# A convolution and attention stack on one Trainium2 core: feature tiles that rotate, images held as halves, and convolution dealt out by counted TensorE time

## The chip, the cores and the metric

The kernel runs on one core of a Trainium2 chip. The metric is the device time of one execution in microseconds. It is a single program with hand-ordered instruction streams: every engine executes its own instructions in the order in which the program emits them, and semaphores join the engines.

## The reference

The input `x` is 8 images of 32 x 32 pixels with 256 channels, in float32. Two layers follow.

Layer 0 normalises each image over 32 groups of channels and adds to `x` the concatenation of a 3 x 3 convolution (192 channels) and of attention with 8 heads of size 8 (64 channels). The logits have two relative terms, one by row and one by column, which come from tables of 63 vectors:

```python
logits = einsum('bnid,bnjd->bnij', q, k) + rel_w + rel_h      # 1024 x 1024 for each of 8 heads
attn   = einsum('bnij,bnjd->bnid', softmax(logits), v)
x      = x + concat(conv3x3(gn(x)) + conv_b, attn @ attn_w + attn_b)
```

Layer 1 normalises each token, adds single-head attention over the 1024 tokens (`U = 128`), normalises again, and adds a mixture of experts. Its router uses the mean over an image's normalised tokens, so that each image picks two of eight experts (256 to 512 to 256, exact gelu), followed by a layer norm.

```python
t = t + (softmax(Q K^T / sqrt(128)) V) W_o + b_o + ln(t)
t = t + ln(experts(ln(t), top 2 of softmax(mean(ln(t)) @ Wr + br)) + ln(t)) * gamma + beta
```

## The kernel before

The tokens of an image are held as 8 tiles of 128 tokens (`NT`). The first phase, some 2050 us long, does layer 0 and the attention of layer 1 for the eight images in a software pipeline. The second phase, from about 2060 us to the end, does the router and the experts, and the change does not touch it.

**Features.** Layer 0's attention is computed from 128-row feature tiles. The product of a key matrix `KM` (keys, and constant rows that pick a row and a column) with a feature tile `F` gives logits that contain both relative terms and minus the row maximum. `F` is a 2 MB tile put together by DMA from DRAM scratch: `fd` holds the queries and the column pieces, `fy` the row pieces. There are three buffers for such tiles, `F0`, `F1` and `F2`, each with room for one. They also serve as scratch for the queries (`scr`, in `queries`, L534 to L546) and for the normalised tokens, queries and keys of layer 1 (`nqk`, in `Second`).

**Units.** An image has four units (`Unit`): head group `g` by half of the queries. A unit loads `F` (L671 from `fd`, L675 from `fy`, on the SP queue), computes 32 score products (`score`, L690) with a maximum of each on DVE (L697), folds the maxima and sends them by DMA into the rows `R_M` of `F` (`fold`, `fold_in` L713, `fold_out` L724 on ACT's queue). Then it weighs: 32 products (`weigh`, L734) with an exponential on ACT each (L741), and for every four of them a product with the values (`gather`, L750). `settle` (L765) transposes the result.

**The main loop.** `first_layer(b)` runs over the 32 steps `s` of an image, eight for each unit, with four places `p` each: 128 places, one `weigh` at each. While a unit weighs, the next one scores, 4/3 products a place or 8/5 from place 5 in the last unit, where the next one is unit 0 of the next image. At `s == NT` (place 32) the whole of layer 1's attention of the image before (`second_layer`) runs between two places. `project` prepares it during the first unit.

**Filling.** At each place the loop calls `fill.send(us)`. It runs what was put off by `later` (`catch_up`), then one step of a chain of side work, each step ending in `yield None`, and then convolution matmuls (L625) up to a credit of `us`, each of which is entered at 0.36 us. `pace` divides the convolution still owed by the places left. A convolution belongs to one image and is done by Winograd-like transforms along a row: `combine` (L493 on DVE, L496 on POOL) makes the six transformed inputs `V`, and `convolve_pair` issues 12 matmuls for a pair of them, 72 for an image (two instructions in the trace for each). After a pair, ACT copies the result and DVE or POOL add it to the image tile `T`.

**Side work.** After place 32 the chain holds, in this order: `token_mean(b - 1)` (write of `T` to DRAM, statistics, and the sum of normalised tokens with DVE products L1089 to L1091 and matmuls L1096), `fetch(b + 1)` (load of the next image into `T`, then eight empty steps), and `normalise(b + 1)`. The last transposes the image (L385), takes group statistics, makes `base`, then the keys and queries `kq` (`pk`, L434, with L442 on DVE), splits them into two parts (L428 on ACT, L429 on POOL), writes `kd`, and waits until the loop has reached `s == 2 * NT` (`may_query`). Then come the copies of `queries`, the values (`pvv`, L460), and the relative pieces of `features`: four rows (products `prel`, L566, ACT copy L584, DVE remainder L587, two DMA writes of `fy` L589) alternating with four columns (L603, L604), and then the write of the columns to `fd` (L614). Keys of group 0 (L554) and `Unit(b + 1, 0)` follow. `combine` waits for place 88 (`may_combine`).

**Where each tile lies.** Unit 3 uses `F2`, the others use `F0` or `F1` by parity:

```python
self.F = f_tile("F", 2 if n == 3 else (b + n) % 2)
scr    = f_tile("scr", b % 2)
big    = f_tile("nqk", 2, FP)
```

`Unit(b, 2)` is made at place 32, `Unit(b, 3)` at place 48 (`s == NT + 4`), and `Unit(b + 1, 1)` at place 96.

Of the kernel before, what the change touches and what calls it, by code (L numbers as in the profile page):

```python
# [38 lines left out]
def kernel(  # L39
# [44 lines left out]
    all1 = all1.to_broadcast([P, P])  # L84
# [27 lines left out]
    with ExitStack() as ph:  # L112
# [11 lines left out]
        def load_image(b):  # L124
            t = work.tile([P, NT, C], FP, tag="T", name="T", bufs=2)
            for g in range(2):
                nc.sync.dma_start(
                    out=t[:, 4 * g : 4 * g + 4, :], in_=xt[b, g * 512 : g * 512 + 512].rearrange("(p k) c -> p k c", k=4)
                )
            return t  # L130

        ph.enter_context(tc.manual_schedule())
        T = {0: load_image(0)}
# [79 lines left out]
        nc.vector.tensor_copy(kqb, pkb[:, 0:1])  # L213
# [113 lines left out]

        class Fill:
# [11 lines left out]
            def catch_up(self):  # L340
                due, self.due = self.due, []
                for work in due:
                    work()
# [8 lines left out]
            def send(self, us):  # L352
                self.catch_up()
                self.step()
                self.left += us
# [18 lines left out]
        ready = {}  # L374

        def normalise(b):
# [5 lines left out]
            def turned(kc, g):  # L382
                tp = lg_tile("tpx")
                for k in range(4):
                    nc.tensor.transpose(tp[:, k:512:4], T[b][:, 4 * g + k, kc * P : (kc + 1) * P], ident)  # L385
                return tp

            for kc in range(KC):
                for g in range(2):
                    nc.vector.bn_stats(st[:, kc, g, :], turned(kc, g))  # L390
                    yield None
                nc.vector.bn_aggr(mv[:, kc, :], st[:, kc].rearrange("p q s -> p (q s)"))
# [3 lines left out]
            nc.tensor.matmul(pm[:, 0:KC], lhsT=gavg, rhs=mv[:, :, 0], start=True, stop=True)  # L396
# [9 lines left out]
            nc.tensor.matmul(pv[:, 0:KC], lhsT=gavg, rhs=dm[:, :, 0], start=True, stop=True)  # L406
# [20 lines left out]
            def split(c):  # L427
                nc.scalar.copy(kqh[:, 0, c], kq[:, c])  # L428
                nc.gpsimd.tensor_tensor(kqh[:, 1, c], kq[:, c], kqh[:, 0, c], ALU.subtract)  # L429

            for q in range(2):
                pk = lg_tile("pk")
                for kc in range(KC):
                    nc.tensor.matmul(  # L434
# [7 lines left out]
                nc.vector.tensor_scalar(kq[:, c], pk, kqb, kqs, ALU.add, ALU.mult)  # L442
                fill.later(lambda c=c: split(c))
                yield None
            yield None
            kd = kds[b % 2]
            nc.sync.dma_start(out=kd.rearrange("l p s -> p l s"), in_=kqb_[0:DK])
            ready[b] = kqb_
            yield None
            while b > 0 and (done[b - 1] < NT or not may_query.get(b)):  # L450
                yield None
            qs, qx = queries(b)
            nc.gpsimd.tensor_tensor(T[b], T[b], l0b.to_broadcast([P, NT, C]), ALU.add)
# [3 lines left out]
            pv = mi_tile("pvv").rearrange("p (j c) -> p j c", c=DK)  # L457
            for j in range(NT):
                for kc in range(KC):
                    nc.tensor.matmul(  # L460
                        pv[:, j, :],
                        lhsT=base[kc][:, j * P : (j + 1) * P],
                        rhs=qkvw[:, kc, 2 * DK : 3 * DK],
                        start=kc == 0,
                        stop=kc == KC - 1,
                    )
                if j % 2:
                    yield None
            v0[b] = work.tile([P, NT, DK], FP, tag="v0", name="v0")
            nc.vector.tensor_tensor(v0[b], pv, vb.unsqueeze(1).to_broadcast([P, NT, DK]), ALU.add)  # L470
            yield None
            yield from features(b, qs, qx)
            if b > 0:
                keys(b, 0)
            units[b, 0] = Unit(b, 0)
            while not may_combine.get(b):
                yield None
            yield from combine(b, base)

        may_query, may_combine, units = {}, {}, {}  # L480
# [46 lines left out]
        def queries(b):  # L527
            kqb_ = ready.pop(b)
            scr = f_tile("scr", b % 2).rearrange("p w h s -> p (w h s)")
            qs = scr[:, 0 : 2 * S].rearrange("p (g s) -> p g s", g=NG)  # L530
            qx = scr[:, 2 * S : 4 * S].rearrange("p (g s) -> p g s", g=NG)
            for g in range(NG):
                for i in range(4):
# [25 lines left out]
        def features(b, qs, qx):  # L559


            def piece(tab, src, q):
                pr = lg_tile("prel").rearrange("p (i g s) -> p i g s", g=NG, s=32)
                for n in range(8):
                    i = q * 8 + n
                    nc.tensor.matmul(  # L566
# [29 lines left out]
            def column(q):  # L596
                pr = piece(bws, qx, q)
                for g in range(NG):
# [5 lines left out]
                    fill.later(lambda ps=ps, hi=hi, lo=lo: nc.vector.tensor_tensor(lo, ps, hi, ALU.subtract))  # L604

            for q in range(4):
                row(q)
                yield None
                column(q)
                yield None  # L610
            for g in range(NG):
                dst = fds[b % 2][g][R_M * HG : (R_M + 64) * HG].rearrange("(l p) s -> p l s", p=P)
                for p in (slice(HG, 64), slice(64, P)):
                    nc.sync.dma_start(out=dst[p], in_=whole[g].bitcast(FP)[p])  # L614

        done = {}

        def convolve_pair(b, g, pair):
# [3 lines left out]
            for i, j in enumerate(pair):  # L622
                for dy in range(3):
                    for kc in range(KC):
                        nc.tensor.matmul(  # L625
# [8 lines left out]
            Tg = T[b][:, 4 * g : 4 * g + 4, 0:CO]  # L634
            if pair == (0, 5):
                nc.vector.tensor_tensor(Tg[:, 0:4:3], pc, Tg[:, 0:4:3], ALU.add)
                fill.catch_up()
                done[b] = 4 * g + 4
            else:
                mm = work.tile([P, 2 * CO], FP, tag="n", name="mm", bufs=2).rearrange("p (j o) -> p j o", j=2)  # L640
                nc.scalar.copy(mm, pc)  # L641

                def rest():
                    ms = work.tile([P, CO], FP, tag="ms", name="ms")
                    nc.vector.tensor_tensor(ms, mm[:, 0], mm[:, 1], ALU.add)
                    nc.vector.tensor_tensor(mm[:, 0], mm[:, 0], mm[:, 1], ALU.subtract)
                    sd = (ms, mm[:, 0])
                    if pair == (1, 2):
                        for k in range(2):
                            T2 = Tg[:, k:4:2]  # L650
                            nc.gpsimd.tensor_tensor(T2, T2, sd[k].unsqueeze(1).to_broadcast([P, 2, CO]), ALU.add)
# [221 lines left out]
        def fetch(b):  # L873
            T[b] = load_image(b)
            for _ in range(8):
                yield None
# [546 lines left out]
```

## Time and profile before

| what | value |
| --- | --- |
| median of 3 runs | 2538.64 us (2533.96 to 2553.05) |
| the profiled execution | 2547.53 us, its span 2545.8 us |
| mean granted TensorE clock | 0.916 |
| busy share: PE, DVE, ACT, POOL | 89%, 57%, 40%, 16% |
| DMA moved | 185.97 MB, mean 73 GB/s |
| one steady image (4), from its first weigh to the next image's | 242.6 us |
| its second layer, between places 31 and 32 | 50.1 us |

All times in what follows are microseconds of the profiled execution unless they are called medians. Its own time is 1.7 us more than its span, and 8.9 us more than the median. "Granted clock" is the share of full speed that TensorE's throttle allowed in a stretch. In a table of windows a busy share of PE near the window's length means only that a matmul was in flight: at a clock of 0.5 the same matmul is in flight for twice as long.

### The profile page before, as it was taken

The page shows a single profiled execution, that of the slowest core. Times are in us where ns is not written, and L with a number is a line of the kernel's source. Part 1 is how long each engine was busy: PE and PEld are TensorE (multiplying, and loading weights), DVE is VectorE, ACT ScalarE, POOL GpSimd, SP SyncE. Part 2 cuts the span into 40 slices and gives each one's busy share as a digit, 9 for nine tenths or more (in the row PEclk, how much of TensorE's full clock was granted, in tenths as well). Part 3 has the DMA queues.
Part 4 walks back from the last instruction along what each step waited for, and adds up shares of the span by engine and source line. Part 5 has one row for each costly group of instructions (what it writes and reads, how often), then busy time and mean ns, then how long its engine had stood idle before and what let it go on. Part 6 is the DMA issues. An engine that isn't in the chain of part 4 may idle for free.

```text
span 2545.8 us, 28672 instructions
## 1 busy us (share of the span) xinstructions
PE 2270.9 (89%) x10507; PEld 1455.8 (57%) x10507; DVE 1455.3 (57%) x3229; ACT 1010.4 (40%) x1921; POOL 404.7 (16%) x294
## 2 busy tenths in 40 slices
PE   5479999899989998999899989998998869999998
PEld 4346556556646654566556645655653546666665
DVE  4656766665757576666666666666563443333333
ACT  1144543444434444544443444344445312332222
POOL 2101120211021111201110112021100032222220
PEclk7788999799979997998899889989999879999999
DMA  5543412531271145024512351243120031221110
GB/s 133 120 84 101 91 34 67 134 57 34 70 170 17 34 112 137 10 52 107 123 39 64 95 105 34 67 124 68 34 51 2 0 121 66 75 75 66 66 58 25
DMA packets 91165, 185.97 MB, mean 73 GB/s; under 512 B 9313, under 2 KB 37866, under 8 KB 88466
## 3 DMA queue, kind: packets, MB, share of 16 engines
q1 hardware_dynamic: 89216, 181.55, 29.3%
q10 hardware_dynamic: 1810, 2.59, 0.4%
q8 instruction: 84, 1.38, 0.2%
q14 instruction: 55, 0.45, 0.1%
HBM read 112.15 MB, written 62.52 MB: 69 GB/s over the span
## 4 chain that ended last, share of the span: by engine, by line
PE 70%; DVE 14%; DMA 8%; ACT 3%; SPq 2%; issue 2%; POOL 1%; ACTq 0%; DVEq 0%; POOLq 0%
PE phd L1333 9%; PE py L1350 9%; PE st L734 8%; PE po L750 8%; PE lg L690 8%; PE pc L625 6%; DVE mx L697 5%; PE po L1051 4%; PE lg L973 4%; DMA F<-fy 3%; DMA F<-mb 3%; PE pq L847 2%; PE prel L566 2%; PE tp L997 2%; PE pa L1059 1%
## 5 line engine op out<-in xcount | busy, mean ns | idle before, releaser
L697 DVE TENSOR_REDUCE mx<-lg 128x1 f32<-128x512 f32 x1024 | 660.1, 684 | 375.5 <-PE lg L690 370.6
L741 ACT ACTIVATE PT<-st 128x512 f32<-128x512 f32 x1024 | 590.9, 597 | 572.6 <-PE st L734 518.6
L734 PE MATMUL st<-F,KM 128*128 128x512 f32 x1024 | 536.4, 530 | 55.3 <-ACT PT L741 34.5
L690 PE MATMUL lg<-KM,F 128*128 128x512 f32 x1024 | 400.8, 433 | 68.5 <-DMA F<-fy 64.8
L734 PEld LDWEIGHTS st<-F,KM 128*128 128x128 f32 x1024 | 208.9, 206 | 244.1 <-ACT PT L741 153.8
L750 PE MATMUL po<-PT,vk 128*32 128x512 f32 x2048 | 308.0, 673 | 0.7 <-POOL vk L871 0.7
L625 PE MATMUL pc<-convw,V 128*128 128x192 f32 x1152 | 283.5, 339 | 9.2 <-ACT mm L641 5.0
L625 PEld LDWEIGHTS pc<-convw,V 128*128 128x128 f32 x1152 | 206.2, 193 | 118.5 <-issue 71.4
L690 PEld LDWEIGHTS lg<-KM,F 128*128 128x128 f32 x1024 | 212.8, 208 | 101.1 <-issue 73.0
L1333 PE MATMUL phd<-n2T,w 128*128 128x512 f32 x512 | 225.4, 596 | 0.0
L1350 PE MATMUL py<-w,hT 128*128 128x256 f32 x1024 | 223.6, 379 | 0.0
L1350 PEld LDWEIGHTS py<-w,hT 128*128 128x128 f32 x1024 | 194.6, 190 | 33.3 <-issue 7.7
L1357 DVE TENSOR_TENSOR r<-py,n 128x256 f32<-128x256 f32 x64 | 27.2, 425 | 261.4 <-PE py L1350 261.4
L1333 PEld LDWEIGHTS phd<-n2T,w 128*128 128x128 f32 x512 | 96.2, 191 | 114.0 <-issue 110.3
L978 ACT ACTIVATE pr<-lg,nm 128x512 f32<-128x512 f32 x128 | 86.7, 683 | 127.4 <-DVE nm L975 127.2
L1340 ACT ACTIVATE hT<-phd,b1c 128x512 f32<-128x512 f32 x128 | 86.3, 686 | 96.6 <-PE phd L1333 96.5
L974 DVE TENSOR_REDUCE nm<-lg 128x1 f32<-128x512 f32 x128 | 86.5, 688 | 64.1 <-PE lg L973 64.1
L973 PE MATMUL lg<-nqk 128*128 128x512 f32 x256 | 120.9, 595 | 0.0
L1051 PE MATMUL po<-pt,v 128*128 128x256 f32 x512 | 115.8, 379 | 0.0
L429 POOL TENSOR_TENSOR kqh<-kq,kqh 128x512 fp32r<-128x512 f32 x16 | 20.4, 1275 | 557.6 <-ACT kqh L428 557.5
L828 POOL TENSOR_TENSOR T<-T,n 128x256 f32<-128x256 f32 x64 | 48.5, 777 | 369.0 <-DVE n L827 369.0
L1051 PEld LDWEIGHTS po<-pt,v 128*128 128x128 f32 x512 | 95.1, 190 | 11.6
(249 smaller groups left out, 2462.6 us busy)
## 6 DMA issues: line engine op xcount, KB each, us to landing
F<-fd SPq DMA_DIRECT2D x64, 768.0 KB
fy<-rel SPq DMA_DIRECT2D x64, 256.0 KB
F<-fy SPq DMA_DIRECT2D x128, 128.0 KB
w<-in_L_ffn_W_dram SPq DMA_DIRECT2D x32, 512.0 KB
T<-in_x_dram SPq DMA_DIRECT2D x16, 512.0 KB
scr<-kqh SPq DMA_DIRECT2D x64, 128.0 KB
fd<-kqh SPq DMA_DIRECT2D x32, 256.0 KB
fd<-rel SPq DMA_DIRECT2D x16, 512.0 KB
```

The source lines that it names most:

```text
L625: nc.tensor.matmul(pc[:, i], lhsT=V[j][:, kc, (16 * g + dy) * NQ : (16 * g + dy) * NQ + P], rhs=convw[:, j, dy * KC + kc], start=dy + kc == 0,
L690: nc.tensor.matmul(lg, lhsT=self.F[:, a, hl, i * P : (i + 1) * P], rhs=KM[:, self.g * HG + hl, a * 512 : (a + 1) * 512], start=True, stop= ...
L697: nc.vector.tensor_reduce(self.mx[:, a, i, hl : hl + 1], lg, AX.X, ALU.max, negate=True)
L734: nc.tensor.matmul(st, lhsT=KM[:, self.g * HG + hl, j * P : (j + 1) * P], rhs=self.F[:, j // 4, hl, :], start=True, stop=True,)
L741: nc.scalar.activation(self.pts[j][:, hl, :], st, AF.Exp)
L750: nc.tensor.matmul(self.po[32 * hl : 32 * hl + 32, :], lhsT=vk[:, j, (self.g * HG + hl) * (DH + 1) : (self.g * HG + hl) * (DH + 1) + 32], ...
L973: nc.tensor.matmul(lg[h], lhsT=q, rhs=k[:, h * 512 : (h + 1) * 512], start=True, stop=True)
L974: nc.vector.tensor_reduce(nm[:, h : h + 1], lg[h], AX.X, ALU.max, negate=True)
L978: nc.scalar.activation(pr[:, h * 512 : (h + 1) * 512], lg[h], AF.Exp, bias=nm[:, 2:3], scale=scale, accum_out=rs[:, h, i : i + 1],)
L1051: nc.tensor.matmul(po[:, 0:IB], lhsT=sec.v[:, jc, :], rhs=pt[:, jc, :], start=jc == 0, stop=jc == NT - 1)
L1333: nc.tensor.matmul(phd, lhsT=ws[k][0][:, kc, f * P : (f + 1) * P], rhs=n2T[:, kc, q * 512 : (q + 1) * 512], start=kc == 0, stop=kc == KC - 1,)
L1350: nc.tensor.matmul(py, lhsT=hT[:, k * NF + f, j * P : (j + 1) * P], rhs=ws[k][1][:, f, :], start=k + f == 0, stop=k == TOPK - 1 and f == N ...
```

## The change

1. **Roles rotate.** Of the three feature buffers, `place_of(b, role)` gives role 0 (scratch of the queries, units 0 and 2), role 1 (units 1 and 3) and role 2 (`nqk` of the image before) to another buffer in each image. The scratch for the next image's queries is thereby the buffer that `nqk` leaves at place 32. The waits `may_query` and `may_combine` go: the queries follow at once when the keys are made, and `combine` waits only until the image before has its convolution done. `Unit(b, 3)` is made at place 64, where unit 1 leaves its buffer, with the next image's keys of group 0 behind it. The score schedule follows: unit 3 is scored at 15/8 a place from place 7 of unit 2 on, and the next image's unit 0 at 11/8 from place 1 of unit 3 on.
2. **Halves.** `T` becomes two tiles of four token tiles each, with two buffers a half. The first half of the image after next is loaded when `token_mean` of half 0 is done, inside the second layer. `token_mean` runs once for each half, the first inside the second layer. Its constant term goes into the first DVE product in place of a matmul.
3. **Pieces.** The order is row, column, column, row, column, column, row, write of the columns, an empty step, last row, where rows and columns alternated. Two empty steps stand ahead of the first piece. The values use two `lg` tiles and not the convolution's `mi` tile.
4. **Counting.** `Counted` adds an estimate of TensorE's time for every matmul and transpose. `send(us, level)` gives the convolution the credit `level + us - spent`. The convolution is paced to end at place 66 of the image's own loop.
5. **Smaller moves.** The scaling of `kq` and one copy of `nqk` go from DVE to ACT, with the split in the same step. The copies of the queries are issued replica by replica. Adding a pair (3, 4) to `T` is spread over three sends.

```diff
+        class Counted:
+            spent = 0.0
+            def matmul(self, out, **kw):
+                n = math.prod(out.shape[1:])
+                us = max(n * (0.00046 if kw["rhs"].dtype == FR else 0.00168), 0.06)
+                self.spent += 0.31 * us if out.shape[0] == 32 else us
+                nc.tensor.matmul(out, **kw)
+            def transpose(self, out, in_, ident):
+                self.spent += 0.115
+                nc.tensor.transpose(out, in_, ident)
...
+        def load_half(b, g):
+            t = work.tile([P, 4, C], FP, tag=f"T{g}", name="T", bufs=2)
...
+        def place_of(b, role):
+            return (role - b) % 3
...
-            def send(self, us):
+            def send(self, us, level=None):
                 self.catch_up()
                 self.step()
-                self.left += us
+                self.left += us if level is None else max(level + us - te.spent, 0.0)
+                te.spent = 0.0
...
-                nc.vector.tensor_scalar(kq[:, c], pk, kqb, kqs, ALU.add, ALU.mult)
-                fill.later(lambda c=c: split(c))
+                nc.scalar.activation(kq[:, c], pk, AF.Identity, bias=kqb, scale=kqs)
+                nc.scalar.copy(kqh[:, 0, c], kq[:, c])
+                nc.gpsimd.tensor_tensor(kqh[:, 1, c], kq[:, c], kqh[:, 0, c], ALU.subtract)
...
-            while b > 0 and (done[b - 1] < NT or not may_query.get(b)):
-                yield None
             qs, qx = queries(b)
...
-            if b > 0:
-                keys(b, 0)
             units[b, 0] = Unit(b, 0)
-            while not may_combine.get(b):
+            while b > 0 and done[b - 1] < NT:
                 yield None
             yield from combine(b, base)
...
-            scr = f_tile("scr", b % 2).rearrange("p w h s -> p (w h s)")
+            scr = f_tile("scr", place_of(b, 0)).rearrange("p w h s -> p (w h s)")
...
-            for g in range(NG):
-                for i in range(4):
+            for i in range(4):
+                for g in range(NG):
...
-            for q in range(4):
-                row(q)
-                yield None
-                column(q)
-                yield None
+            for f, q in ((row, 0), (column, 0), (column, 1), (row, 1), (column, 2), (column, 3), (row, 2)):
+                f(q)
+                yield None
+            store_columns()
+            yield None
+            yield None
+            row(3)
+            yield None
...
-                self.F = f_tile("F", 2 if n == 3 else (b + n) % 2)
+                self.F = f_tile("F", place_of(b, n % 2))
...
-                big = f_tile("nqk", 2, FP).rearrange("p w h s -> p (w h s)")
+                big = f_tile("nqk", place_of(b + 1, 2), FP).rearrange("p w h s -> p (w h s)")
...
-        def fetch(b):
-            T[b] = load_image(b)
-            for _ in range(8):
+        def fetch(b, g, wait):
+            load_half(b, g)
+            for _ in range(wait):
                 yield None
...
-        def pace(b, s, p):
-            if done.get(b, NT) < NT:
-                left, later = 4 * (15 - s) - p, 5.0 if s < NT else 0.0
-            else:
-                left, later = 4 * (32 - s) - p + 24, 5.0
-            return max(fill.owed - later, 0.0) / max(left, 1)
+        LAST = 66
+        def pace(b, place):
+            left = (LAST if done.get(b, NT) < NT else 128 + LAST) - place
+            return fill.owed / max(left, 1)
...
+            starts = {2: lambda p: (p - 7) * 15 // 8, 3: lambda p: (p - 1) * 11 // 8}
+            starts[0] = starts[1] = lambda p: p * 4 // 3 + 1
...
                     if more:
-                        fill.chains.append(fetch(b + 1))
+                        fill.chains.append(fetch(b + 1, 1, 3))
                         fill.chains.append(normalise(b + 1))
-                elif s == NT + 4:
+                elif s == 2 * NT:
                     units[b, 3] = Unit(b, 3)
-                elif s == 2 * NT:
-                    may_query[b + 1] = True
-                elif s == 2 * NT + 6:
-                    may_combine[b + 1] = True
+                    if more:
+                        assert b + 1 in kept
+                        keys(b + 1, 0)
...
-                    fill.send(pace(b, s, p) * (0.6 if p == 1 else 1.13))
+                    fill.send(pace(b, 4 * s + p), 0.7)
...
+                    if ib % 2:
+                        fill.chains.append(token_mean(b, ib // 2, st2))
+                        if ib == 1 and b + 2 < B:
+                            fill.chains.append(fetch(b + 2, 0, 0))
...
-        def token_mean(b):
+        def token_mean(b, half, st2):
...
```

## The prediction

> **What bounds the kernel now.** I read the page first, then TensorE's timeline of one steady image cut at its score matmuls, then waits and the SP queue inside the bad stretches. From the page:
>
> ```profile
> PE 2270.9 (89%) x10507; PEld 1455.8 (57%) x10507; DVE 1455.3 (57%) x3229; ACT 1010.4 (40%) x1921; POOL 404.7 (16%) x294
> PEclk7788999799979997998899889989999879999999
> PE 70%; DVE 14%; DMA 8%; ACT 3%; SPq 2%; issue 2%; POOL 1%; ACTq 0%; DVEq 0%; POOLq 0%
> ```
>
> TensorE bounds it, but about every third slice its clock sags, and 8% of the chain is DMA. L734 runs 1024 times, 128 an image: I call each one a place. Image 4 lasts from 1034.3 to 1276.9, 242.6 us. Windows cut at places 0, 31, 32 (between them the second layer), 53, 64, 72, 81, 89, 96, 104 and 128; columns are length, then busy PE, PEld, DVE, ACT, POOL, granted clock, DMA share and GB/s:
>
> ```profile
> 1034.30:1082.60 48.30, 45.32 (x243) 27.46 (x242) 32.12 (x77) 24.02 (x47) 11.41 (x11) 1.00 0.08 13
> 1082.60:1132.70 50.10, 49.35 (x241) 36.10 (x240) 29.76 (x63) 19.57 (x50) 2.00 (x2) 1.00 0.22 43
> 1132.70:1161.30 28.60, 24.04 (x113) 14.97 (x112) 21.12 (x55) 12.78 (x24) 0.00 (x0) 0.88 0.57 147
> 1161.30:1173.70 12.40, 12.06 (x78) 7.22 (x76) 10.57 (x29) 6.16 (x14) 0.00 (x0) 1.00 0.01 4
> 1173.70:1187.80 14.10, 14.10 (x81) 9.01 (x79) 9.08 (x16) 6.78 (x12) 2.55 (x2) 1.00 0.28 62
> 1187.80:1213.80 26.00, 23.36 (x104) 17.62 (x103) 12.96 (x24) 9.13 (x19) 8.36 (x3) 0.64 0.49 128
> 1213.80:1223.30 9.50, 9.50 (x36) 4.52 (x36) 6.19 (x11) 4.71 (x10) 0.00 (x0) 0.72 0.79 230
> 1223.30:1232.50 9.20, 5.25 (x28) 1.72 (x27) 6.97 (x14) 4.33 (x8) 6.57 (x8) 1.00 0.89 188
> 1232.50:1246.80 14.30, 9.75 (x32) 4.21 (x33) 4.83 (x10) 4.74 (x9) 2.13 (x3) 0.64 0.94 193
> 1246.80:1276.90 30.10, 29.74 (x162) 19.54 (x161) 23.21 (x44) 14.83 (x27) 2.14 (x2) 1.00 0.14 24
> ```
>
> The reader sees three holes. Just after place 32, 4.6 us idle and a clock of 0.88 (the token mean's DVE burst). In places 72 to 89 the relative pieces run at 0.64 and 0.72. In 89 to 104 TensorE is idle 8.5 us while DMA is 0.9 busy. Busy time by clock over 960 to 1200 adds up to 202 of 240 us; 20 are idle, 18 are lost to the clock. Only these 38 us an image can be won. The waits from place 72 to 128 name what ends the last hole:
>
> ```profile
> PE lg L690 <- DMA F<-fy: 4.5, 1, 4.5
> PE st L734 <- DMA F<-mb: 2.6, 1, 2.6
> ```
>
> The SP queue shows why the features of the next image come so late: copies of the queries, relative pieces and both loads of F follow each other within 60 us.
>
> ```profile
> 1182.33 0.60 SPq L447 DMA_DIRECT2D kd<-kqh  x1
> 1183.03 6.98 SPq L534 DMA_DIRECT2D scr<-kqh  x8
> 1190.06 3.23 SPq L541 DMA_DIRECT2D fd<-kqh  x4
> 1216.09 4.78 SPq L614 DMA_DIRECT2D fd<-rel  x4
> 1224.87 8.12 SPq L671 DMA_DIRECT2D F<-fd  x2
> 1233.04 2.53 SPq L675 DMA_DIRECT2D F<-fy  x4
> ```
>
> **The change, stage by stage, one image.** I count the sends of the chain of side work, one a place. After place 32: five of the mean of half 1, load and three waits, then normalise. That puts the two key and query matmuls (pk) at places 52 and 53, the queries' copies at 55, the pieces at 59 to 65 and 68, and F of the next image's unit 0 at 69. Before, pk stands at 64 and 65, the pieces at 73 to 80, that F at 82. Thirteen places earlier; the price is that F of unit 3 is now asked for at place 64 and not 48, and that its scores (32 between places 72 and 89) meet the combination for the convolution, which now starts at 69 and not 88.
>
> *Places 0 to 31 and the second layer, 98.4 us.* TensorE is 94.7 busy at clock 1.00. Two copies of 0.69 us go from DVE to ACT, whose idle time covers them. Half 0's mean (4 products of 0.48 us, 4 aggregates, the inverse root) enters the second layer, where DVE has 20 us free; if a matmul waits for it, about 1 us. I take +1: 99.4.
>
> *32 to 53, 28.6 us.* Half 1's mean has half the DVE work: 4 x 0.15 + 4 x 0.48 us less, so ACT gets its inverse root about 2 us earlier and the 4.6 us hole closes to about 2, with less of the 2.9 us of lost clock. More convolution moves in: today image 4 has 30, 30, 26, 0 and 58 of its 144 instructions in 0-31, second layer, 32-64, 64-104 and 104-128; spread evenly some 6 matmuls of 0.32 us come here. Between 23.5 and 28; I take 25.5.
>
> *53 to 72, 26.5 us.* This stage gets dearer. From the second pk (1177.54) to the first piece (1192.28) took 14.7 us: product, split, then 9 to 10 us of SP issues and copies. That path stays, less one late send. TensorE has between them pk 1.9, five places of 0.24 to 0.55, 3.3 of pvv, 1.1 of po, 0.5 of pmx and about 4 convolution matmuls: some 10.4 us. So it waits 4 us, where it waited 2.1, and again 1.5 us for POOL's second copy (1.96 us each, both now start at the end of the copies). Eight pieces then cost 0.9 us each at full clock and 1.75 at half. With weigh, gather and ACT's 0.6 us a place, 72 is reached 43 us after 53 at half clock. At full clock it would be 31, but then F of unit 3, asked for about 23 us after 53 and 11.0 to 11.25 us in transfer (the two cold loads on the chain), holds the first score until 35. So 35 to 43. The wait before the pieces resembles the one that took the clock down in image 3, nearer the half-clock row:
>
> ```profile
> 960.00:965.00 5.00, 5.00 (x24) 3.66 (x17) 1.63 (x5) 1.18 (x2) 0.00 (x0) 0.50 0.11 38
> 965.00:970.00 5.00, 5.00 (x20) 4.51 (x20) 2.69 (x6) 1.18 (x3) 0.00 (x0) 0.50 0.33 108
> 970.00:975.00 5.00, 5.00 (x18) 2.50 (x18) 2.40 (x5) 2.33 (x6) 0.00 (x0) 0.50 0.47 148
> ```
>
> I take 38, as some places lie between the pieces now. (The Trainium skill, page TensorE: Matmul & The Clock Gate, section "Part 1: The HAM clock gate", says that one idle window of about 3.4 us halves the clock and one busy window of that length restores it. Its first half speaks against this change, which lengthens the wait at the first piece; its second half disagrees with these rows, where PE is fully busy for 15 us and stays at 0.50. By the rule the stage would be about 35 us and the kernel some 20 us faster than my sum; I follow the rows.)
>
> *72 to 89, 35.5 us.* The pieces are gone. DVE sets the pace: 32 maxima of 0.64 back to back are 20.5 us, the combination about 10.5 us (its 14 operations in image 4 last 0.42 to 0.94 us), of which 3 places fall before 72. 27 to 31; I take 29.5. TensorE's 17 places (some 17 us with 1.9 scores each, and convolution) hide under it.
>
> *89 to 96, 9.2 us.* The maxima's DMA (mb) meets a quieter queue: next F is asked for at 69, and 5.5 MB lie before it at about 200 GB/s, so it lands some 39 us after place 64; place 92 comes at about 43. ACT's 7 x 0.6 us and convolution: 6. *96 to 104, 14.3 us:* the wait for F goes, 8 places of about 1 us: 8. *104 to 128, 30.1 us:* 29 matmuls of convolution become about 11, 18 x 0.32 us less: 24.
>
> Sum 99.4 + 25.5 + 38 + 29.5 + 6 + 8 + 24 = 230.4, that is 12.2 us less an image, 85 for the seven that prepare a successor. Against it image 0: its successor's input is asked for behind a 2 MB F at place 32 and wanted at 35, not 43; 3 MB take about 14 us by the 11 us row, places 3 to 4: +9. At the end only half a mean is left: -4, half of the stretch 2040 to 2048. The renamed roles themselves, the flush, and 16 ACT products in place of DVE's cost nothing visible (ACT is 40% busy; without that cover 0.6 us each, 10 us). The profiled execution took 2547.5 us (span 2545.8), so 2467; the median of the runs is 8.9 lower: **about 2457 us**.
>
> **Rivals.** *All holes close.* If the convolution that is left fills the wait at place 58, the pieces keep the clock, and F of unit 3 is there at 72: 99 + 24 + 31 + 25.5 + 5.5 + 8 + 23 = 216, 26.6 less, so about 2360. For it: TensorE would be at 202 + 14 of real work, and 29 places lie between the request and the need of the next image's first F. Against: no work is put before the first piece on purpose, and unit 3's F has only 8 places.
>
> *Gain eaten.* The counter subtracts also the convolution sent at the place before, so credit comes only at every second place and what is left piles up before place 66, at half clock: the count does not spread evenly. If 53 to 89 takes 43 + 34 and the rest is as above, 240 an image: about 2530.
>
> *Slower.* One mechanism: the load of F for unit 3, on SP behind the writes of pieces 0 and 1, which wait for DVE, and sharing the DMA engines with 2.5 MB of pieces. TensorE is in order, so its first score at place 72 stops the weighing behind it, ACT then starves, and the combination is late next. In the forecast F lands 11 us after place 64. From about 12 us beyond that the gain is gone; at 17 us beyond (3 MB of other traffic ahead) an image costs 247, about 2575. For it: F<-fd took 8.12 us to issue twice and landed late when it followed the pieces. Against: there it waited for its own data, here the data lie in DRAM since the image before.
>
> **How the numbers follow.** Forecast (2415 to 2510) 0.55; all holes close (2340 to 2415) 0.18; gain eaten (2513 to 2564) 0.15; slower 0.12. One per cent, 25 us, is about what a measurement here can tell from no change. Faster 0.73, same 0.15, slower 0.12. The range 2375 to 2540 takes in the bounds of places 53 to 89 (35 to 43, 27 to 31) and leaves about 0.2 out.
>
> **What would show it.** Right: an image period near 230; no wait of lg for F<-fy at places 98 to 104; mb landing in 2 to 3 us; pieces some 13 places earlier, still with clock about 0.5; a wait of prel near 4 us; about two thirds of the convolution gone from 104 to 128 to other stages. Wrong: a clock near 1.0 through the pieces (then faster), or a wait of lg for F above 10 us in places 72 to 76 (then no gain).

## The result, and the profile after

The changed kernel takes 2648.25 us (median of 4 runs, 2638.23 to 2652.23) against 2544.52 for the kernel before: 1.040 times the time, 95% interval 1.035 to 1.046. The forecast was 2457 us. The kernel is about 104 us slower, and it was to be 87 us faster.

The page of the changed kernel (its profiled execution took 2638.23 us), the rows that answer to the three shown of before:

```profile
PE 2269.2 (86%) x10507; PEld 1450.2 (55%) x10507; DVE 1424.8 (54%) x3269; ACT 1035.4 (39%) x1969; POOL 396.2 (15%) x302
PEclk7796999799989988998899799989999879999999
PE 60%; DVE 22%; DMA 8%; ACT 3%; issue 3%; SPq 2%; ACTq 1%; POOL 1%; DVEq 0%; POOLq 0%
```

TensorE has the same matmuls and is busy for as long, so the 90 us of added span are idle time of TensorE. Image 4 of the changed kernel runs from 1081.1 to 1335.6, 254.5 us where it was 242.6. The same kind of windows, here cut at places 0, 31, 32, 53, 64, 72, 89, 96, 104 and 128:

```profile
1081.10:1130.30 49.20, 45.29 (x233) 26.58 (x233) 30.73 (x75) 24.62 (x47) 11.41 (x11) 0.97 0.07 12
1130.30:1187.10 56.80, 52.04 (x248) 37.97 (x246) 32.58 (x78) 20.38 (x52) 2.00 (x2) 0.97 0.25 56
1187.10:1217.30 30.20, 26.08 (x134) 15.52 (x133) 25.22 (x67) 13.07 (x26) 0.00 (x0) 0.94 0.11 36
1217.30:1249.10 31.80, 26.18 (x131) 18.96 (x129) 8.67 (x18) 11.40 (x21) 10.86 (x6) 0.72 0.44 104
1249.10:1269.80 20.70, 12.35 (x62) 8.32 (x63) 4.32 (x11) 6.87 (x14) 0.00 (x0) 0.75 1.04 244
1269.80:1293.90 24.10, 22.24 (x88) 11.04 (x88) 23.71 (x43) 10.20 (x18) 7.48 (x10) 0.87 0.57 133
1293.90:1302.10 8.20, 6.89 (x40) 3.45 (x38) 3.49 (x8) 3.77 (x7) 0.00 (x0) 1.00 0.01 4
1302.10:1310.40 8.30, 8.30 (x47) 5.40 (x48) 4.99 (x11) 5.83 (x11) 1.15 (x1) 1.00 0.87 200
1310.40:1335.60 25.20, 24.62 (x134) 14.79 (x132) 19.16 (x36) 14.02 (x25) 1.00 (x2) 1.00 0.15 20
```

Against the forecast: 106.0 for 99.4 up to place 32, 30.2 for 25.5, **52.5 for 38** in places 53 to 72, 24.1 for 29.5, 8.2 for 6, 8.3 for 8, and 25.2 for 24. Together the image misses its 230.4 us by 24.1. The late gains came for the most part (places 89 to 128 are down from 53.6 to 41.7, forecast 38). Two losses were not foreseen. Row five shows the first: 8.3 us of idle PE with DMA at 1.04. The waits of places 53 to 72, of PE and then of ACT, name it:

```profile
PE st L132 <- ACT PT L768: 8.4, 1, 8.4
PE prel L132 <- DMA scr<-kqh: 4.7, 1, 4.7
ACT rel L606 <- DMA fy<-rel: 9.1, 1, 9.1
```

Line 132 is the counting helper, so tiles tell the instructions apart. L606 is ACT's copy of a row piece. Its buffer is one of the three of `b_tile`, and `base` holds the other two, so the copy of row 3 waits until the write of row 2 has landed. The exponentials (L768) stand behind that copy, and TensorE waits for them. The SP queue shows what that write waits for:

```profile
1248.86 1.27 SPq L698 DMA_DIRECT2D F<-fd  x2
1250.17 2.71 SPq L702 DMA_DIRECT2D F<-fy  x4
1252.92 1.04 SPq L576 DMA_DIRECT2D KM<-kd  x2
1257.68 2.42 SPq L611 DMA_DIRECT2D fy<-rel  x2
1260.60 3.51 SPq L632 DMA_DIRECT2D fd<-rel  x4
```

Unit 3's F (L698, L702, 2 MB) and the keys are issued from 1248.86, and row 2's write (L611) at 1257.68, behind them. On the chain of work that ended last this is, in each of images 1 to 6, 10 to 11 us of F<-fd and then 7 to 9 us of fy<-rel. Where nothing stands ahead of it, the same write is 2.5 us on the chain (kernel before, at 57.69).

The second loss is in the second layer, 56.8 for 50.1 us. Its longest wait of PE is for half 0's sum:

```profile
PE pmean L132 <- DVE acc L1117: 2.8, 1, 2.8
```

### The profile page after: what moved, and what is told of

Same layout as the page of the kernel before. It is cut to its first block, busy times and chain, and to the rows that moved or that the text cites. A ratio compares the mean times of both kernels' runs of the same rounds, so it can differ in the third digit from the quotient of the medians.

```text
span 2636.4 us, 28742 instructions
## 1 busy us (share of the span) xinstructions
PE 2269.2 (86%) x10507; PEld 1450.2 (55%) x10507; DVE 1424.8 (54%) x3269; ACT 1035.4 (39%) x1969; POOL 396.2 (15%) x302
## 4 chain that ended last, share of the span: by engine, by line
PE 60%; DVE 22%; DMA 8%; ACT 3%; issue 3%; SPq 2%; ACTq 1%; POOL 1%; DVEq 0%; POOLq 0%
DVE mx L724 11%; PE po L132 11%; PE phd L1357 8%; PE py L1374 8%; PE lg L132 8%; PE st L132 7%; PE pc L132 4%; DMA F<-fd 3%; PE pq L132 2%; PE prel L132 2%; DMA fy<-rel 2%; PE tp L136 2%; SPq L556 1%; DVE V L515 1%; DMA F<-fy 1%
## 5 line engine op out<-in xcount | busy, mean ns | idle before, releaser
L768 ACT ACTIVATE PT<-st 128x512 f32<-128x512 f32 x1024 | 595.3, 597 | 521.5 <-PE st L132 480.5
L132 PE MATMUL st<-F,KM 128*128 128x512 f32 x1024 | 528.5, 521 | 76.8 <-ACT PT L768 75.9
L132 PEld LDWEIGHTS st<-F,KM 128*128 128x128 f32 x1024 | 202.8, 199 | 302.0 <-ACT PT L768 216.6
L132 PE MATMUL po<-PT,vk 128*32 128x512 f32 x2048 | 297.7, 653 | 0.0
L132 PEld LDWEIGHTS lg<-KM,F 128*128 128x128 f32 x1024 | 200.9, 197 | 136.0 <-issue 63.7
L132 PEld LDWEIGHTS pc<-convw,V 128*128 128x128 f32 x1152 | 215.4, 199 | 69.9 <-issue 23.9
L132 PE MATMUL po<-pt,v 128*128 128x256 f32 x512 | 129.8, 412 | 0.0
L132 PEld LDWEIGHTS po<-pt,v 128*128 128x128 f32 x512 | 105.6, 211 | 15.6
L609 DVE TENSOR_TENSOR rel<-prel,rel 128x512 fp32r<-128x512 f32 x32 | 22.1, 691 | 168.7 <-ACT rel L606 168.7
```

Source lines behind the costliest of these rows:

```text
L132: nc.tensor.matmul(out, **kw)
L768: nc.scalar.activation(self.pts[j][:, hl, :], st, AF.Exp)
```

## Experiments

Times of whole kernels are medians; each group ran beside its own runs of the kernel before (2541 to 2547 us). "A", "B" and "C" are the theory and its rivals in the text that stands ahead of each result. Images are numbered from 0.

**The load behind row 2's write.** `Unit(b, 3)` and the keys are made by the chain of pieces and not at the top of place 64:

```diff
+            if b > 0:
+                while not free.get(b - 1):
+                    yield None
+                units[b - 1, 3] = Unit(b - 1, 3)
+                keys(b, 0)
             store_columns()
...
-                    units[b, 3] = Unit(b, 3)
...
+                    free[b] = True
...
```

> The changed kernel with one step moved: F of unit 3 (and the keys behind it) is asked for two places later, behind the write of row piece 2 and ahead of the write of the columns. Theory A (order in the queue): in the changed kernel ACT's copy of row piece 3 waits 9.1 us for the buffer of row piece 2, whose write stands behind the 2 MB load of F; the exponentials queue behind that copy and TensorE starves. Then places 64 to 72 fall from 21 to 12 to 14 us, 72 to 89 rise by at most 3 (F lands later), an image costs 247 to 250 in place of 253 to 254, and the kernel 2590 to 2620 us. Rival B (DMA engines full): the engines are busy all through that stretch (share 1.04), so whatever goes first something else is late by as much; TensorE then waits for F at place 72 and the time stays within 10 us of the changed kernel's 2648.

2638 us. In image 4 places 64 to 72 fell to 13.5 us as A has it, and ACT's longest wait for fy<-rel fell from 9.1 to 2.1. But 72 to 89 rose to 36.2, with a new wait:

```profile
PE lg L132 <- DMA F<-fy: 11.1, 1, 11.1
```

So the order moves the wait and does not remove it, as B says for the time. B's reason does not hold: the DMA share there is 0.38 and then 0.77, not full. Asked for at place 64 or later, the load is late in either order.

**No load for unit 3.**

```diff
-                self.F = f_tile("F", place_of(b, n % 2))
+                self.F = units[b, 1].F if n == 3 else f_tile("F", place_of(b, n % 2))
...
+                if n != 3:
...
```

The loads of L698 and L702 stand under this `if`. The kernel leaves out unit 3's load, and with it that load's 2 MB of traffic.

> The changed kernel, where unit 3 loads no F: it scores and weighs with unit 1's tile, so its logits are those of other queries and the computation of that unit is changed. Theory A (the load asked for at place 64 and needed at 72 is too late, in whatever order it stands): without it ACT's wait of 9.1 us goes and no wait for F takes its place; places 64 to 72 take 11 to 13 us and 72 to 89 24 to 26, an image 244 to 247, the last one 193 to 196, the kernel 2575 to 2600 us. Rival B (the pieces' own cost, the wait for the queries' copies and half clock): 64 to 72 still takes 16 us or more, the kernel 2615 us or more.

2556 us, 93 less. Image 4 takes 239.6 us (images 1 to 6: 239.6 to 247.4), the last one 195.6 to its last weigh (204.7 before the edit; there unit 3's first score waited 7.0 us for F). By A, with somewhat more than it gave: ACT's longest wait for fy<-rel in image 4's stage is 2.9 us, and no score waits for F there.

**The old roles.** Buffers, unit 3 at place 48, start of the queries, place of the keys and pace of scoring as before:

```diff
-                self.F = f_tile("F", place_of(b, n % 2))
+                self.F = f_tile("F", 2 if n == 3 else (b + n) % 2)
...
-            starts = {2: lambda p: (p - 7) * 15 // 8, 3: lambda p: (p - 1) * 11 // 8}
+            starts = {2: lambda p: p * 4 // 3 + 1, 3: lambda p: (p - 5) * 8 // 5 + 1}
...
```

> The changed kernel with the roles of the feature buffers, the request for unit 3's F at place 48, the start of the queries at place 64, the place of the keys and the pace of scoring as they were before; halves, order of the pieces, count and the smaller moves stay. Theory A (the rotation is what hurts; the count is worth 25 to 40 us, half 0's mean costs 40): 2535 to 2565 us, 64 to 72 at 14 and 72 to 89 at 28 to 36. Rival B (halves and pieces hurt as much): 2600 us or more.

2501 us, ratio to before 0.985 (0.982 to 0.989). This group of edits, called the rotation below, costs 147 us; all the other parts together are a gain of 42. The time is below A's lower end. Its windows for places 64 to 72 and 72 to 89 of image 4 tell why:

```profile
1159.20:1173.90 14.70, 14.70 (x104) 11.31 (x105) 9.16 (x18) 6.77 (x15) 8.30 (x4) 1.00 0.76 180
1173.90:1195.30 21.40, 19.70 (x112) 11.79 (x111) 19.35 (x36) 12.40 (x26) 6.30 (x9) 1.00 0.68 190
```

The pieces stand here, at places 68 to 77, and the clock is 1.00. In the kernel before, these windows took 14.1 us at 1.00 and 35.5 us at 0.64 to 0.72.

**The remaining 55 us of the rotation.** Four kernels without unit 3's load. First, four more empty sends ahead of the first piece (`range(2)` to `range(6)`):

> The kernel without unit 3's load of F (that unit's logits are therefore those of other queries), with six empty sends in place of two between the values and the first relative piece. Without the four further sends TensorE waits 4.5 us for the copies of the queries at place 59 and the first pieces run at half clock (places 53 to 64 take 29 us at a clock of 0.83). Theory A (the queries' copies follow the keys too closely, with nothing left to score): the wait goes, 53 to 72 falls from 41 to 34 to 37 us, and the kernel from 2556 to 2505 to 2535. Rival B (the pieces themselves hold the clock down): 53 to 72 stays above 39 and the kernel within 15 us of 2556.

2580 us, dearer by 25: both missed. In image 3 PE still waits 3.8 us at the first pieces (1.8 for the copies, 2.0 for POOL), and all pieces but one run at half clock; in image 4, with nearly the same waits (1.8 and 1.7), only one does in full (1.92 us, the next 1.26). The chain is four places longer. Then the queries' copies held to place 64 (`while b > 0 and not may_query.get(b): yield None`), and the same with unit 3 scored at 4/3 from place 64:

> The kernel without unit 3's load of F (that unit's logits are those of other queries), with the start of the queries' copies held to place 64, as in the kernel before; keys are still made at places 52 and 53. Theory A (the 54 us that the rotation costs beyond that load come from the queries' copies right behind the keys, with TensorE out of score products): no wait of the first piece for the copies, 53 to 89 falls from 64 us to 50 to 56, the kernel from 2556 to 2495 to 2525. Rival B (the pieces go at half clock wherever no scores stand beside them, places 57 to 72): the wait goes but the clock in 64 to 72 is 0.5 to 0.7, the kernel 2535 to 2585.

> The kernel of the run before this one, with unit 3 scored at 4/3 a place from place 64 on, which it can be since it loads nothing. Theory A: little changes, within 15 us of the run before. Rival B (scores beside the pieces keep the clock): the clock in 64 to 89 is above 0.95 where the run before had less, and the kernel is 25 us or more below it, 2490 to 2515.

2575 and 2567 us. B by the time in the first, but the wait had not gone, which neither had: 4.8 and 3.1 us at the first piece. In the second pair A is near (8 us), and scores beside the pieces do not keep the clock. On SP the copy of the keys (L578, 0.5 MB) stood ahead of the queries' copies (L558), and it had two waits of its own, for `kd` and for the weighing that still read the old keys:

```profile
SPq L578 <- DMA kd<-kqh: 3.7, 1, 3.7
SPq L578 <- PE st L132: 2.7, 1, 2.7
1190.79 0.61 SPq L468 DMA_DIRECT2D kd<-kqh  x1
1197.90 0.80 SPq L578 DMA_DIRECT2D KM<-kd  x2
1198.74 6.21 SPq L558 DMA_DIRECT2D scr<-kqh  x8
```

So the queries' copies left at 1198.74, 0.8 us after place 64. The last kernel moves only the copy of the keys, behind the pieces:

```diff
-                    if more:
-                        assert b + 1 in kept
-                        keys(b + 1, 0)
...
+            if b > 0:
+                keys(b, 0)
             units[b, 0] = Unit(b, 0)
```

> The kernel of no_f_query64_scores (unit 3 loads no F, its logits are those of other queries) with the copy of the next image's keys issued behind the pieces, ahead of F of the next unit 0, and not at place 64 ahead of the queries' copies. Theory A (a wait of about 3 us at the first piece is what takes the clock down for all of them): the wait falls below 1.5 us, the clock in places 64 to 89 is above 0.93, 64 to 89 falls from 50 to 36 to 40 us, the kernel from 2567 to 2480 to 2510. Rival B (the buffers' roles cost in some other way): the kernel stays above 2540.

2519 us, 48 less, by A (a little short of its range). The queries' copies now follow the write of `kd` at once, 6.4 us ahead of place 64 (1169.0), although the program emits them at that place:

```profile
1161.95 0.61 SPq L468 DMA_DIRECT2D kd<-kqh  x1
1162.65 7.65 SPq L560 DMA_DIRECT2D scr<-kqh  x8
```

Windows of places 64 to 72 and 72 to 89, image 4, with the keys ahead:

```profile
1197.90:1220.30 22.40, 19.30 (x107) 14.90 (x107) 10.27 (x20) 7.51 (x15) 8.41 (x4) 0.80 0.64 141
1220.30:1247.80 27.50, 26.60 (x111) 16.34 (x111) 18.35 (x34) 12.30 (x24) 6.06 (x8) 0.73 0.52 153
```

and with the keys behind:

```profile
1169.00:1183.90 14.90, 14.90 (x107) 11.75 (x107) 9.22 (x18) 7.45 (x15) 8.45 (x4) 1.00 0.56 134
1183.90:1205.20 21.30, 19.65 (x112) 11.85 (x111) 19.26 (x36) 11.91 (x24) 6.10 (x8) 1.00 0.66 188
```

The same matmuls to within a few instructions, 49.9 us in the one and 36.2 in the other. The wait at the first piece, 3.1 us in the one, is not in the other's list, and the clock goes from 0.80 and 0.73 to 1.00. Of these 13.7 us an image keeps 5.8: places 89 to 104 rise from 16.9 to 22.2, with F of the next unit 0 later, and those up to place 32 from 106.0 to 108.6. So of the 147 us the load is 93. The last three edits together (the copies held, the scoring, the keys behind) are 37, and what they end in is a first piece without a wait and pieces at full clock. 18 us are left to the other edits in that group, not separated.

**Half 0's mean.** Put off until the second layer is over:

> The changed kernel with the token mean of half 0 (and the load of the next image's first half behind it) put off until the second layer is over, as both halves were before. Theory A: the second layer's 56.8 us (50.1 before) come from TensorE waiting 2.8 us for the sum of half 0 and from what that wait takes from the clock; the second layer returns to 50 to 52, places 32 to 53 rise from 30 to 33 to 36, and the kernel gains 0 to 20 us. Rival B: the second layer is longer because of where convolution and the half loads now fall; it stays at 55 to 57 and the kernel gets 20 to 40 us slower, since the side chain is longer by six places.

2641 us: in image 3 the second layer returns from 57.6 to 50.4 us as in A, and 32 to 53 rises to 33. The kernel gains 7 us, in A's range but hardly more than its runs scatter: with the chain longer by six places, image 3 gives the 7.2 us back (1.6 up to place 31, 2.8 in 32 to 53, 2.4 in 53 to 89, 2.5 in 89 to 96). Instead, two empty sends between the DVE products and the matmul:

```diff
             del T[b][half]
             yield None
+            for _ in range(0 if half else 2):
+                yield None
```

> The changed kernel with two more sends between the DVE products of the mean of half 0 and the matmul that sums them, so that TensorE meets the matmul when the sum is there. Theory A: the wait of 2.8 us and the clock it costs are what makes the second layer 6 us longer; it falls to 51 to 53 and the kernel gains 25 to 45 us, 2603 to 2625. Rival B: the second layer is longer by the DVE work that the half brings into it (about 4 us) and stays at 54 or more, the kernel gains under 15 us.

2620 us, 28 less: image 4's second layer takes 52.2 us at clock 1.00 where it had 0.97, and no wait for the sum is left. A, by the time. With the old roles as well, and then with the two sends for half 1 too:

> The kernel of the run before this one with the two further sends ahead of the matmul of half 0's mean. Theory A: the second layer returns to 51 to 53 us, and the kernel takes 2495 to 2520, below before and level with before plus the count alone (2507). Rival B: the two sends change nothing, within 10 us of the run with the roles alone undone.

> The kernel with the old roles and two further sends ahead of the sum of half 0 (2446 us), with the two sends for half 1 as well. Theory A: the wait of 2.3 us behind place 32 goes as the one in the second layer did, 32 to 53 falls by 2 to 4 us an image, 2420 to 2440. Rival B: the chain is two places longer, the keys come closer to the copies, and it is no faster, 2440 to 2460.

2446 us, 55 less than the old roles alone and more than A gave; and 2442, only 4 less, since in image 4 32 to 53 falls by 4 us but 53 to 72 rises by 5: the wait goes as in A, the time is B's.

**The count.** Taken out of the changed kernel, and put alone into the kernel before:

```diff
-                    fill.send(pace(b, 4 * s + p), 0.7)
+                    fill.send(pace(b, 4 * s + p) * (0.6 if p == 1 else 1.13))
```

> The changed kernel with the credit of before (pace times 0.6 or 1.13) in place of the counted one; its last place stays 66. Theory A: the count moves convolution between places but not the stalls, so the time stays within 15 us of the changed kernel's 2648. Rival B: the count is what hurts, since it puts convolution where TensorE is full or at half clock; without it 2560 to 2610 us.

> The kernel before with the counted credit alone (level 0.7, its own pace and last place). Theory A: within 15 us of before, 2530 to 2560. Rival B: the count alone costs 30 us or more, 2575 and up. Rival C: the count alone is a gain of 20 us or more that the other parts hide, 2525 or less.

2673 us (24 more, outside what either theory gave), and 2507 us (ratio 0.985, 0.982 to 0.988): C. The count is a gain, alone and in company.

**Order of the pieces, and early keys.** The old alternating order in the kernel with the old roles; and, on the kernel before with the count, four empty sends behind the image's load in place of eight:

> The kernel with the old roles (2501 us), with the relative pieces also in the old order: row and column in turn, the write of the columns right behind. Theory A (what makes the stage of the pieces 13 us shorter than in the kernel before is that the keys are made twelve places ahead of the queries' copies, not the order): 2495 to 2520. Rival B (the order and the empty sends do it, since ACT no longer waits for a write of fy): 2560 or more, and the clock in the stage falls to 0.7.

> The kernel before with the counted credit (2507 us) and one number changed: four empty sends behind the load of the next image in place of eight, so that its keys are made four places earlier, while the queries' copies still wait for place 64. Theory A: the first piece no longer waits for the copies, the pieces keep the clock near 1.0, places 72 to 89 fall from 35 to 22 to 27 us, the kernel to 2430 to 2465. Rival B (the halves are needed for it, or the input arrives too late): 2490 or more.

2484 us, below A's range: the new order costs 17, and A is right that the order does not make the stage short (B is out). And 2477 us, 29 less than with the count alone but short of A's 2430 to 2465. In image 3 places 72 to 89 fell from 35.7 to 22.5 us, but 64 to 72 rose from 14.1 to 19.2: the first piece still waited 2.3 us, and the first four ran at half clock (1.75 to 1.89 us each against 0.97 to 1.08).

**The parts that gain, together.** Old roles, old order, two sends for both halves; count, halves and smaller moves stay:

> Old roles, the pieces in the old order, two further sends ahead of the sums of both halves; count, halves and the smaller moves stay. Theory A: the parts add up, 2484 - 59 or so, 2415 to 2435, the fastest of all. Rival B: each closes the same holes, 2440 to 2455.

2428 us, ratio to before 0.954 (0.951 to 0.958), ahead of both kernels, by A. Its page has the clock nearly whole (mean 0.970; 0.921 in the changed kernel):

```profile
PE 2161.9 (89%) x10507; PEld 1386.4 (57%) x10507; DVE 1425.8 (59%) x3269; ACT 1031.4 (43%) x1969; POOL 399.9 (17%) x302
```

## Why the prediction was wrong

*The step that failed is the stage of places 53 to 72*, bounded at 35 to 43 and measured at 52.5 in image 4 (49.8 to 53.3 in images 1 to 6). The text counted each transfer of the moved load, but priced it only as a wait at the first score of unit 3. It gave the writes of the pieces, which share the queue with that load, no wait at all. In fact row 3's copy needs the one free buffer, its release hangs on a write queued behind the 2 MB load, and ACT's exponentials hang on the copy: 8.4 us of idle TensorE on top of the 43 of its own half-clock bound. The trace of before has a smaller wait of the same kind, which the prediction did not use (image 3, ACT's copies of rows):

```profile
ACT rel L584 <- DMA fy<-rel: 3.6, 2, 3.4
```

*The rival "slower" named the right transfer* but gave it 0.12, and it put the wait in the wrong place: in image 4 no score waits for F between places 72 and 89, and the sign that it gave for "no gain" (a wait of lg for F above 10 us) shows only when the load is moved behind row 2. It argued that the data of unit 3's F lie ready since the image before; that is true and beside the point, because the request comes 8 places before the need (64 for 72) in place of 16 (48 for 64, where before's trace has unit 3's first score). The later request was costed as a neutral move; without the load the kernel is 93 us faster. That is the cost of the load as it stands. Whether its place in the queue or the full DMA engines (share 1.04) delay the write was not separated, and a fourth buffer for the row copies, or their writes on another queue, was not tried.

*The second layer*: +1 us was taken for half 0's mean ("about 1 us, if a matmul waits for it"); it measured +6.1 to +6.7, of which 4.6 went with two empty sends. The mis-sized term is the wait and its clock: 2.8 us idle and a clock of 0.97 over 57 us. *32 to 53*: 30.2 for 25.5; the hole did not close (4.1 us idle where it was 4.6), since a matmul waits 2.3 us for the second half's sum. *72 to 89*: 24.1 for 29.5, taken too dear.

*What was right:* the places of the pieces (59 to 65 and 68), the wait for the queries' copies at place 59 (4 us forecast, 4.7 measured), F of the next unit 0 in time, and maxima back in time. The convolution left the last stage only in part: 16 matmuls stay there, 29 before and 11 in the forecast.

*The clock:* the forecast took 38 us, between 35 at full clock and 43 at half, and named pieces at a clock of about 0.5 as a sign. In image 4 six of the eight pieces run at half clock (1.75 to 1.92 us), the seventh takes 1.24 and the last 0.97; images 1 and 5 are like it. In images 2, 3 and 6 only the first two run at half clock (1.89 to 1.92 us), the others take 0.97 to 1.16. Yet their stage is hardly shorter (49.8 to 51.0 us), for there ACT waits 12.9 to 13.9 us for row 2's write where it waits 7.1 to 9.1 in the others. So the load and the write behind it set the end of the stage at either clock. The Trainium skill's page TensorE: Matmul & The Clock Gate, section "Part 1: The HAM clock gate (the "warmup" mystery)", says that an idle window of about 3.4 us throttles and a busy one restores. The waits of 4.7 us here agree with the first half; but the clock also fell behind 3.1 us (keys ahead of the queries' copies) and behind 2.1 us (image 4 of the kernel before). For the second half the runs show both: a recovery after two pieces in three images here, none for six pieces in three others with the same wait, and the kernel before at 0.50 for 15 us of busy PE. What decides between them was not tried.

The rival "gain eaten" blamed the count; the count gains 24 to 37 us.

## What to carry to other kernels

When a request is moved later, price it twice: at its consumer, and at everything that is queued behind it, then follow the buffers that those transfers release and the engines that wait for these buffers. A matmul that needs a sum should be issued when the sum is there: in an in-order stream two empty steps ahead of half 0's sum were worth 28 to 55 us (ahead of half 1's only 4, since the chain behind it grew). A copy that has to wait holds up all that stands behind it in its queue, so put it behind what is wanted first. When a change has several parts, run each alone: here four parts gained 42 us together, the fifth lost 147, and the best set of them is 4.5% faster than before.

## What the runs showed of the hardware

A wait of about 3 us at the head of a stage of short matmuls came with a loss far above itself. With the keys ahead of the queries' copies on one queue, the first piece waited 3.1 us, the granted clock was 0.5 from 1211.3 to 1235.2, and 17 places took 27.5 us at a clock of 0.73; with the keys behind, they took 21.3 us at 1.00. Over the kernel one reordered copy was worth 48 us. The size of the wait alone does not tell how long the clock stays down: behind 4.7 us it came back after two pieces in three images of the changed kernel and after six or more in three others.

A queue of DMA issues stops at a copy that waits: with the keys ahead, the queries' copies left 0.8 us after place 64, and with the keys behind 6.4 us before it.

A write of 0.5 MB queued behind a load of 2 MB on the same queue landed late although their data have nothing to do with each other: 7 to 9 us more on the chain, after 10 to 11 us of the load, where the same write is 2.5 us with nothing ahead of it.
